# A GRU, convolution and mixture-of-experts kernel: the convolution in 16 pieces with four buffers, and the experts' down products next to the following pair's gate and up products

## The chip, the core and the metric

The kernel runs on one core of a Trainium2 chip. The metric is the device time of one execution in microseconds (us); three runs of the kernel before took 2714.86 to 2716.25 us, with a median of 2714.9 us.

## What is computed

The input x is 128 sequences (b) of 64 steps (t) of 512 features, and cond is 128 rows of 512. Two residual layers follow one another:

```python
# layer 0: a GRU over t that starts from cond, then a linear layer with
# weights rounded to -1, 0, 1 times one scale
x = x + ffn0(gru(cond, x))
# layer 1: a depthwise causal convolution of x along t whose taps are the
# 128 rows of cond, then a mixture of experts with a shared expert
h = conv(x, cond[:, None, :]) + bias
scores = softmax(h @ gate_w.T)              # 64 experts, the best 6 of each row
y = sum over chosen experts of score * ((silu(h @ w_gate[e]) * (h @ w_up[e])) @ w_down[e])
x = x + y + (silu(h @ sw_gate) * (h @ sw_up)) @ sw_down
```

Each expert keeps only the first 64 of the 8192 rows that chose it (CAP); an expert's inner width is 352, the shared expert's is 704. All data are float32.

## The kernel before

TensorE (PE) runs through five stages one after the other.

**The recurrence** (the loop over t at L444). In each step PE multiplies the state by the recurrent weights (L457), adds the input gates of later steps from a stream of products that needs the input weights wih and the bias bi (L311, Strassen-like products for two steps at a time), and applies the rounded linear layer to the state of the step before (ffn, L383). ffn adds the result to x (L398), and SyncE (SP) stores this x1 twice: into out (L408) and into x1c (L400), a scratch array in DRAM ordered as [slice of features][time, reversed][b][features of the slice]. DS is the number of features in one half of a slice, and a row of x1 goes to x1c in runs of DS numbers. In the steps from 2 on, toeplitz (L127) lays out the taps of one half slice in a second scratch array, tzd. The input weights, bi and the other weights are in one pool of on-chip memory, w0, which lives until the loop's end.

**The convolution** (L538 to L574). It is a product of x1c with a Toeplitz matrix of the taps, slice by slice: 8 slices (NSL) of 2 x 32 features. A slice needs two tiles: xc, 2 MB of x1c, and tz, 1 MB of tzd, the two halves of whose partitions are loaded by two DMAs (load_toeplitz, L139, one on SP's queue and, except for slice 1, one on ScalarE's (ACT's)); the rest of tz is cleared once by GpSimd (POOL) (clear, L118). There are two pairs of such tiles, used in turn. The first is made at the start; its first slice is loaded within the recurrence, late rows at step 61 (L406 and L410). The second pair is made after the recurrence, in memory that the recurrence's pools have given up (L535). A slice has 8 groups of 8 matmuls with 64 columns of stationary data each (conv_group, L155); VectorE (DVE) evicts a group with two additions of the bias into hid (L554). Four groups of slice 0 are computed before the last steps of the recurrence are through (L489 to L497). The last two time steps enter by another way: tail_products (L528) and an addition per slice on DVE (L566), from tiles xl and tap that POOL loads. After slice 6, and after slice 7, SP stores the first four steps of hid to the table tab (L573).

**Routing and the shared expert's first half** (L917 to L1024), then **slot counting** (L1098), then **the routed experts together with the shared expert's second half** (L1303 to L1322). In this last stage the shared expert's work comes as a stream of small pieces, and after each of them as many pieces of the routed experts follow as a counter makes due (L1317). Experts are taken in 32 pairs; expert_pair (L1227) has four pieces a pair:

- inputs: the pair's gathered rows are transposed on PE (L1241) and copied by DVE to xeT;
- gate and up: 8 matmuls each into pg and pu (L1253), 64 columns of stationary data for one expert, 64 for the other; ACT's silu and DVE's products make a (L1262); POOL issues the gather of the pair after next (L1216);
- turn: a is transposed on PE (L1267) and copied to aeT;
- down: 6 matmuls into py (L1277), again in halves of 64 columns; ACT copies py to ys (L1285, two buffers), and POOL adds ys to out by two scatters (L1287), the second of which waits until the first has landed.

load_expert (L1065) loads wg, wu and wd of the following pair on SP's queue, which is in order; four experts have buffers. SP also loads xr, the shared expert's rows, after POOL's additions to out (L914) have let its buffer go (L1042).

What a queue does first is set by a scheduler that follows program order and the waits of each tile, and that can move an instruction past others; the order that it made is read from the built program.

Of the kernel before, what the change touches and what calls it, by code (L numbers as in the profile page):

```python
# [8 lines left out]
F32 = mybir.dt.float32  # L9
# [10 lines left out]
P = 128  # L20
B = 128
# [11 lines left out]
DS = 32  # L33
# [9 lines left out]
def adaln_ffn_kernel(  # L43
# [78 lines left out]
    conv_buffers(0)  # L122
# [4 lines left out]
    def toeplitz(q):  # L127

        i = nc.sync.dma_start(
            out=tzd[q],  # L130
            in_=bass.AP(taps.tensor, taps.offset + q * DS * 2 * T, [[1, T], [2 * T, DS], [1, T]]),
        )
        tc.keep_in_program_order(i)

        nc.sync.dma_start(
            out=x1c[q, :TAIL].rearrange("s (r b) e -> (s r) (b e)", r=8), in_=zrow[: 8 * TAIL, :D]
        )

    def load_toeplitz(sl):  # L139

        for hf, queue in enumerate((nc.sync, nc.sync if sl == 1 else nc.scalar)):
            queue.dma_start(out=tzs[sl % 2][hf * T : (hf + 1) * T, hf], in_=tzd[2 * sl + hf])

    TAIL = 2
    LAST = 16

    def load_early(sl):
        for hf in range(2):
            nc.sync.dma_start(
                out=xcs[sl % 2][hf * T + LAST : (hf + 1) * T], in_=x1c[2 * sl + hf, LAST:]  # L150
            )
# [3 lines left out]
    def conv_group(sl, g, ps, parts=2):  # L155
# [3 lines left out]
        for j in range(4):  # L159
            for r in range(parts):  # L160
# [3 lines left out]
                    xcs[sl % 2][:, rows, g * 4 + j],  # L164
                    tzs[sl % 2][:, :, g * 4 + j, :],
# [14 lines left out]
    with (  # L180
# [29 lines left out]
        scale = w0.tile([P, 1], F32, name="scale")  # L210

        bi = w0.tile([P, 3 * D], F32, name="bi")
        wih = [w0.tile([P, KD, D], F32, name=f"wih{c}") for c in range(3)]
# [28 lines left out]
        zrow = w0.tile([NPAD, TW], F32, name="zrow")  # L242
# [4 lines left out]
        ones = w0.tile([P, P], F32, name="ones")  # L247
# [6 lines left out]
        def prepare(c):  # L254
# [4 lines left out]
            t1 = w0.tile([P, HK, HD], F32, name=f"t1{c}")  # L259
            nc.vector.tensor_sub(t1, w12, w11)  # L260
            t2 = w0.tile([P, HK, HD], F32, name=f"t2{c}")
            nc.vector.tensor_sub(t2, w22, t1)
            nc.vector.tensor_sub(w12, w22, w12)
            t4 = w0.tile([P, HK, HD], F32, name=f"t4{c}")
# [118 lines left out]
        def ffn(t, pieces):  # L383
# [20 lines left out]
            if t == T - 1 - TAIL:  # L404
                for hf in range(2):
                    nc.sync.dma_start(out=xcs[0][hf * T : hf * T + LAST], in_=x1c[hf, :LAST])  # L406

            (nc.gpsimd if t >= T - TAIL else nc.sync).dma_start(out=out_t[t], in_=x1)  # L408
            if t == T - 1 - LAST:
                load_toeplitz(0)  # L410
                load_early(0)
# [12 lines left out]
        part = w0.tile([P, T], F32, name="part")  # L424
# [3 lines left out]
        total = w0.tile([P, 1], F32, name="total")  # L428
# [4 lines left out]
        half = w0.tile([P, 1], F32, name="half")  # L433
        nc.vector.tensor_scalar(half, scale, EPS, 0.5, ALU.add, ALU.mult)
        nhalf = w0.tile([P, 1], F32, name="nhalf")
# [8 lines left out]
        for t in range(T):  # L444
# [4 lines left out]
            if t == 1:  # L449
                clear(0)  # L450
            if 2 <= t < 2 * NSL + 2:
                toeplitz(t - 2)
            ps_g = []
# [81 lines left out]
    conv_buffers(1)  # L535
    clear(1)
    cb_h = cb.rearrange("p (q h d) -> p q h d", h=2, d=DS)
    with tc.tile_pool(name="ps_c", bufs=4, space=PSUM) as ps_c:  # L538
        for sl in range(NSL):

            if sl >= 1:
                load_toeplitz(sl)
            if sl >= 1:
                nc.sync.dma_start(
                    out=xcs[sl % 2], in_=x1c[2 * sl : 2 * sl + 2].rearrange("h s b e -> (h s) b e")
                )
# [15 lines left out]
            if sl >= 1:  # L562
                if sl == 1:
                    tail_products()
                d = slice(0 if sl == 1 else 2 * DS * sl, 2 * DS * (sl + 1))
# [4 lines left out]
            if sl >= NSL - 2:  # L570
                d = slice(0, 2 * DS * (NSL - 1)) if sl == NSL - 2 else slice(2 * DS * (NSL - 1), D)
# [493 lines left out]
    def load_expert(e):  # L1065
        wex = wexs[e % 4]
        wg = wex.tile([P, KD, EI], F32, name="wg")
        load_rows(wg, w_gate[e])
        wu = wex.tile([P, KD, EI], F32, name="wu")
        load_rows(wu, w_up[e])  # L1070
        wd = wex.tile([P, len(ech), D], F32, name="wd")
        load_rows(wd[:, :efull, :], w_down[e, : efull * P, :])
        nc.sync.dma_start(out=wd[:n_last, efull, :], in_=w_down[e, efull * P :, :])
        return wg, wu, wd

    weights = {e: load_expert(e) for e in range(4)}
# [150 lines left out]
    def expert_pair(q):  # L1227

        for e in (2 * q + 2, 2 * q + 3):
            if 4 <= e < NE:  # L1230
                weights[e] = load_expert(e)
        rows = gathered.pop(q)
        ws = [weights.pop(2 * q + j) for j in range(2)]


        rw = ex.tile([P, 1], F32, name="rw")
        for j in range(2):
            nc.vector.tensor_copy(rw[halves[j]], rows[halves[j], D + 2 * q + j : D + 2 * q + j + 1])
        ps = ps_e.tile([P, D], F32, name="py").rearrange("p (k b) -> p k b", k=KD)
        for k in range(KD):  # L1240
            nc.tensor.transpose(ps[:, k, :], rows[:, k * P : (k + 1) * P], ident)  # L1241
        xeT = ex.tile([P, KD, P], F32, name="xeT")
        nc.vector.tensor_copy(xeT, ps)
        yield

        if q + 2 < NPAIR:
            gathered[q + 2] = gather(q + 2)
        pg = ps_e.tile([P, EI], F32, name="pg")
        pu = ps_e.tile([P, EI], F32, name="pu")
        for which, acc in ((0, pg), (1, pu)):  # L1250
            for k in range(KD):
                for j in range(2):
                    nc.tensor.matmul(  # L1253
                        acc[halves[j]],
                        xeT[:, k, halves[j]],
                        ws[j][which][:, k, :],
                        start=(k == 0),
                        stop=(k == KD - 1),
                    )
        a = ex.tile([P, EI], F32, name="a")  # L1260
        nc.scalar.activation(a, pg, AF.Silu)
        nc.vector.scalar_tensor_tensor(a, a, rw, pu, ALU.mult, ALU.mult)  # L1262
        yield

        ps = ps_e.tile([P, D], F32, name="py").rearrange("p (k b) -> p k b", k=KD)
        for c, (i0, n) in enumerate(ech):
            nc.tensor.transpose(ps[:n, c, :], a[:, i0 : i0 + n], ident)  # L1267
        aeT = ex.tile([P, len(ech), P], F32, name="aeT")
        nc.vector.tensor_copy(aeT[:, :efull, :], ps[:, :efull, :])
        nc.vector.tensor_copy(aeT[:n_last, efull, :], ps[:n_last, efull, :])  # L1270
        yield


        py = ps_e.tile([P, D], F32, name="py")
        for c, (i0, n) in enumerate(ech):
            for j in range(2):
                nc.tensor.matmul(  # L1277
                    py[halves[j]],
                    aeT[:n, c, halves[j]],
                    ws[j][2][:n, c, :],  # L1280
                    start=(c == 0),
                    stop=(c == len(ech) - 1),
                )
        ys = ex.tile([P, D], F32, name="ys")
        nc.scalar.copy(ys, py)  # L1285
        for j in range(2):
            nc.gpsimd.indirect_dma_start(  # L1287
                out=out,
                out_offset=bass.IndirectOffsetOnAxis(
# [82 lines left out]
```

## Time and profile before

| | |
|---|---|
| median of 3 runs | 2714.9 us |
| the profiled execution's own time | 2715.43 us |
| its span | 2713.7 us |
| recurrence, up to PE's last product of ffn | 0 to 1413.5 us |
| convolution, up to PE's last psc | to 1503.4 us |
| routing, shared expert's first half, slot counting | to the first pair's pg at 2071.4 us |
| routed experts with the shared expert's second half | to 2636 us |
| rest of the shared expert | to the end |
| mean granted clock of PE | 0.994 |

The span runs from the first to the last instruction of the profiled execution. In a row of the timeline stand the start, the time from the first start to the last end, engine, line, operation, what is written and what is read, the form and the count; in brackets is the idle time of the engine before it and what ended it. A float32 matmul gives two records, so x64 is 32 matmuls. In a row of the windows there follow on the stretch and its length the busy time (and count) of PE, PEld (weight loads of PE), DVE, ACT and POOL, then PE's granted clock as a share of full speed, the mean busy share of the 16 DMA engines, and the GB/s that they moved.

### The profile page before, as it was taken

Reading aid. Unit: us, or ns where it says so; the run is one execution under the profiler, and the core shown is the slowest. Engines: PE = TensorE matmul, PEld = TensorE weight load, DVE = VectorE, ACT = ScalarE, POOL = GpSimd, SP = SyncE. Lnnn points to the kernel's source line nnn. Section 1 sums busy time; section 2 is a strip of 40 time slices with the busy share of each in tenths; the row PEclk is TensorE's granted clock in tenths of the full one; section 3 lists DMA queues with packets and bytes.
Section 4 is the critical chain, followed back from the end, with each engine's and each line's share of the span. In section 5 each row is a group of like instructions: output and inputs, shape, how many; then the busy total and the mean of one; then the engine's idle time right before and its main releaser. Section 6 shows DMA issues by size and latency. Waiting matters only on the chain. (4 is left out here: it accounts for less than half of the span.)

```text
span 2713.7 us, 31088 instructions
## 1 busy us (share of the span) xinstructions
PE 2664.6 (98%) x11935; PEld 1827.5 (67%) x11935; DVE 1416.9 (52%) x3143; ACT 426.3 (16%) x794; POOL 425.1 (16%) x471
## 2 busy tenths in 40 slices
PE   8999999999999999999997999999999999999999
PEld 5666666666666666666667767777876666666667
DVE  6555555555555555555555755556564333433334
ACT  1111111111111111111110222222221111111111
POOL 2111111111211111111110000000002222222120
PEclk9999999999999999999998999999999999999999
DMA  5323221111211111311148631222256898998962
GB/s 190 89 71 87 75 66 51 43 51 43 57 53 47 51 43 51 66 51 46 52 112 265 248 94 22 41 58 59 61 174 178 274 321 236 316 322 259 284 181 47
DMA packets 329363, 328.02 MB, mean 121 GB/s; under 512 B 184384, under 2 KB 250432, under 8 KB 327040
## 3 DMA queue, kind: packets, MB, share of 16 engines
q1 hardware_dynamic: 302672, 255.52, 30.9%
q0 software_dynamic: 25984, 66.86, 10.5%
q10 hardware_dynamic: 560, 3.67, 0.6%
q8 instruction: 94, 1.54, 0.2%
q14 instruction: 53, 0.43, 0.1%
HBM read 239.73 MB, written 94.65 MB: 123 GB/s over the span
## 5 line engine op out<-in xcount | busy, mean ns | idle before, releaser
L457 PE MATMUL psgh<-whh,hT 128*128 128x512 f32 x1536 | 674.6, 595 | 0.7 <-ACT hT L372 0.7
L457 PEld LDWEIGHTS psgh<-whh,hT 128*128 128x128 f32 x1536 | 286.6, 190 | 350.2 <-issue 336.3
L311 PE MATMUL psx<-wih,xp 128*128 128x256 f32 x768 | 198.5, 381 | 6.8 <-DMA wih<-in_w_ih_dram 6.6
L200 POOL DMA_DIRECT2D xn<-in_x_dram x61 | 34.0, 558 | 853.4 <-DVE x L398 841.8
L311 PEld LDWEIGHTS psx<-wih,xp 128*128 128x128 f32 x768 | 143.7, 191 | 26.5 <-issue 6.6
L467 DVE TENSOR_TENSOR n<-psgh,bhn 128x512 f32<-128x512 f32 x64 | 44.3, 692 | 175.5 <-PE psgh L457 175.5
L372 ACT COPY hT<-psf 128x512 f32<-128x512 f32 x64 | 37.5, 586 | 584.8 <-PE psf L366 584.8
L464 DVE TENSOR_TENSOR r<-psgh,gi 128x512 f32<-128x512 f32 x64 | 44.3, 692 | 139.2 <-PE psgh L457 139.2
L386 POOL TENSOR_TENSOR xn<-xn,fb 128x512 f32<-128x512 f32 x64 | 80.8, 1264 | 143.9 <-DMA xn<-in_x_dram 143.9
L311 PE MATMUL psz<-wih,xs 128*128 128x256 f32 x384 | 98.7, 379 | 1.8 <-DVE gi L334 1.8
L311 PE MATMUL psy<-t,xs 128*128 128x256 f32 x384 | 99.9, 383 | 0.1
L311 PE MATMUL psw<-wih,xp 128*128 128x256 f32 x384 | 99.4, 381 | 0.0
L311 PE MATMUL psw<-t,xp 128*128 128x256 f32 x384 | 98.8, 380 | 0.4 <-DVE u L332 0.4
L311 PE MATMUL psz<-t,xs 128*128 128x256 f32 x384 | 98.7, 379 | 0.0
L390 PE MATMUL psf<-sgn,hhi 128*128 128x512 f32 x256 | 95.2, 493 | 0.0
L1277 PE MATMUL py<-wd,aeT 128*64 128x512 f32 (+1 forms) x384 | 90.6, 601 | 0.0
L1262 DVE SCALAR_TENSOR_TENSOR a<-a,rw,pu 128x352 f32<-128x352 f32 x32 | 18.6, 581 | 136.8 <-PE pu L1253 136.8
L162 PE MATMUL psc<-tz,xc 128*64 128x128 f32 x960 | 68.2, 310 | 20.6 <-DMA xc<-x1c 17.8
L326 DVE TENSOR_TENSOR p<-psx,bi 128x512 f32<-128x512 f32 x96 | 66.4, 692 | 37.3 <-PE psx L311 37.0
L1287 POOL DMA_INDIRECT out_dram<-ys,idxp x32 | 45.5, 1421 | 250.4 <-ACT ys L1285 202.7
L647 PE MATMUL psx<-xr,swg 128*128 128x256 f32 x320 | 84.3, 385 | 0.0
L647 PE MATMUL psx<-hid,swg 128*128 128x256 f32 x320 | 84.1, 386 | 0.1
(298 smaller groups left out, 4672.5 us busy)
## 6 DMA issues: line engine op xcount, KB each, us to landing
wg<-in_w_gate_dram SPq DMA_DIRECT2D x64, 704.0 KB, 8.0
wu<-in_w_up_dram SPq DMA_DIRECT2D x64, 704.0 KB, 10.5
wd<-in_w_down_dram SPq DMA_DIRECT2D x64, 512.0 KB, 8.9
x1c<-x SPq DMA_DIRECT2D x62, 256.0 KB, 4.2
out_dram<-x SPq DMA_DIRECT2D x62, 256.0 KB, 4.5
xn<-in_x_dram POOLq DMA_DIRECT2D x61, 256.0 KB, 4.0
xp<-in_xT_dram POOLq DMA_DIRECT2D x30, 512.0 KB, 4.4
tab<-hid SPq DMA_DIRECT2D x60, 256.0 KB, 3.7
```

The lines of the kernel that those rows point to most:

```text
L162: i = nc.tensor.matmul(ps[rows, j], xcs[sl % 2][:, rows, g * 4 + j], tzs[sl % 2][:, :, g * 4 + j, :], start=True, stop=True,)
L311: i = nc.tensor.matmul(ps, self.ops[n][:, k, :], self.ws[n][:, k, :], start=(first and k == 0), stop=(k == HK - 1), skip_group_check=not f ...
L326: add(self.p1, both, b)
L372: nc.scalar.copy(hT, ps)
L386: nc.gpsimd.tensor_add(xn, xn, fb)
L390: nc.tensor.matmul(ps, piece[:, k, :], sgn[:, k, :], start=(i == 0 and k == 0), stop=(i == 1 and k == KD - 1),)
L457: nc.tensor.matmul(ps, hT[:, k, :], whh[c][:, k, :], start=(k == 0), stop=(k == KD - 1))
L464: nc.vector.tensor_add(r, ps_r, gis.pop((t, 0)))
L467: nc.vector.tensor_add(n, ps_n, bhn)
L647: nc.tensor.matmul(ps.rearrange("p (j b) -> p j b", b=P) if len(r.shape) == 3 else ps, lhs(k), r, start=(first and k == 0), stop=(k == HK ...
L1277: nc.tensor.matmul(py[halves[j]], aeT[:n, c, halves[j]], ws[j][2][:n, c, :], start=(c == 0), stop=(c == len(ech) - 1),)
L1287: nc.gpsimd.indirect_dma_start(out=out, out_offset=bass.IndirectOffsetOnAxis(ap=(idxp[:CAP] if j == 0 else idxo)[:, q : q + 1], axis=0), i ...
```

## The change

The change has two parts that do not touch each other's stages.

First, DS goes from 32 to 16, so there are 16 slices (here "pieces") of half the size, and there are four pairs of tiles (NCB) instead of two, each of half the size. Two pairs are made at the start. The other two are made in step 62 (t == T - TAIL), after a new pool, wi, has been closed that holds bi, the input weights and their sums; other small tiles move ahead of it into w0. Pieces 0 and 1 are loaded as slice 0 was; pieces 2 and 3 are loaded whole at the place where slice 0's late rows are loaded. From piece 4 on load_piece(sl) stands at the start of loop iteration sl, and its tiles are those of piece sl - 4. Stores to x1c have runs of 16 numbers, toeplitz runs in 32 steps instead of 16, the tail's products come with piece 4, and the stores of hid to tab come after pieces 13 and 15.

Second, the pieces of a pair of experts become methods, and experts() orders them anew: turn(q), then inputs(q + 1), then down(q) and gate_up(q + 1) as one piece. Weights of pair q + 2 are loaded in two calls, gate and up in turn(q), down in down(q). The counter spreads 97 pieces over the same stretch of the shared expert as 128 before.

The core of the diff:

```diff
-DS = 32
+DS = 16
...
-    conv_buffers(0)
+    NCB = 4
+    for i in range(2):
+        conv_buffers(i)
...
     def load_toeplitz(sl):
 
-        for hf, queue in enumerate((nc.sync, nc.sync if sl == 1 else nc.scalar)):
-            queue.dma_start(out=tzs[sl % 2][hf * T : (hf + 1) * T, hf], in_=tzd[2 * sl + hf])
+        for hf, queue in enumerate((nc.sync, nc.sync if 2 <= sl < NCB else nc.scalar)):
+            queue.dma_start(out=tzs[sl % NCB][hf * T : (hf + 1) * T, hf], in_=tzd[2 * sl + hf])
...
+    def load_piece(sl):
+        load_toeplitz(sl)
+        nc.sync.dma_start(
+            out=xcs[sl % NCB], in_=x1c[2 * sl : 2 * sl + 2].rearrange("h s b e -> (h s) b e")
+        )
...
+        wi_ = ExitStack()
+        wi = wi_.enter_context(tc.tile_pool(name="wi", bufs=1))
+
+        bi = wi.tile([P, 3 * D], F32, name="bi")
+        wih = [wi.tile([P, KD, D], F32, name=f"wih{c}") for c in range(3)]
...
             if t == T - 1 - TAIL:
-                for hf in range(2):
-                    nc.sync.dma_start(out=xcs[0][hf * T : hf * T + LAST], in_=x1c[hf, :LAST])
+                for sl in range(2):
+                    for hf in range(2):
+                        nc.sync.dma_start(
+                            out=xcs[sl][hf * T : hf * T + LAST], in_=x1c[2 * sl + hf, :LAST]
+                        )
+                for sl in range(2, NCB):
+                    load_piece(sl)
...
             if t == T - 1 - LAST:
-                load_toeplitz(0)
-                load_early(0)
+                for sl in range(2):
+                    load_toeplitz(sl)
+                    load_early(sl)
...
             if t == 1:
                 clear(0)
+                clear(1)
             if 2 <= t < 2 * NSL + 2:
                 toeplitz(t - 2)
+            if t == T - TAIL:
+                wi_.close()
+                for i in range(2, NCB):
+                    conv_buffers(i)
+                    clear(i)
...
-    conv_buffers(1)
-    clear(1)
...
-            if sl >= 1:
-                load_toeplitz(sl)
-            if sl >= 1:
-                nc.sync.dma_start(
-                    out=xcs[sl % 2], in_=x1c[2 * sl : 2 * sl + 2].rearrange("h s b e -> (h s) b e")
-                )
+            if sl >= NCB:
+                load_piece(sl)
...
-            if sl >= 1:
-                if sl == 1:
+            if sl >= NCB:
+                if sl == NCB:
                     tail_products()
...
-            if sl >= NSL - 2:
-                d = slice(0, 2 * DS * (NSL - 1)) if sl == NSL - 2 else slice(2 * DS * (NSL - 1), D)
+            if sl in (NSL - 3, NSL - 1):
+                d = slice(0, 2 * DS * (NSL - 2)) if sl == NSL - 3 else slice(2 * DS * (NSL - 2), D)
...
+    def load_gate_up(q):
+
+        if q < NE // 2:
+            for e in (2 * q, 2 * q + 1):
+                wg = wexs[e % 4].tile([P, KD, EI], F32, name="wg")
+                load_rows(wg, w_gate[e])
+                wu = wexs[e % 4].tile([P, KD, EI], F32, name="wu")
+                load_rows(wu, w_up[e])
+                weights[e] = [wg, wu]
+
+    def load_down(q):
+        if q < NE // 2:
+            for e in (2 * q, 2 * q + 1):
+                wd = wexs[e % 4].tile([P, len(ech), D], F32, name="wd")
+                load_rows(wd[:, :efull, :], w_down[e, : efull * P, :])
+                nc.sync.dma_start(out=wd[:n_last, efull, :], in_=w_down[e, efull * P :, :])
+                weights[e].append(wd)
...
+        pairs = [Pair(q) for q in range(NPAIR)]
+        pairs[0].inputs()
         yield
+        pairs[0].gate_up()
         yield
+        for q, pair in enumerate(pairs):
+            pair.turn()
+            yield
+            if q + 1 < NPAIR:
+                pairs[q + 1].inputs()
+                yield
+            pair.down()
+            if q + 1 < NPAIR:
+                pairs[q + 1].gate_up()
+            yield
...
-            while due < 4 * NPAIR and due * PIECES * SPREAD < slot * 16 * NPAIR:
+            while due < EPIECES and due * PIECES * SPREAD < slot * 4 * EPIECES:
                 next(routed)
                 due += 1
```

The methods of Pair hold the same instructions as the pieces of expert_pair; turn() also calls load_gate_up(q + 2), and down() calls load_down(q + 2) between its products and the copy to ys. EPIECES is 3 * NPAIR + 1.

## The prediction, made before the change was timed

> **What bounds the kernel now.** I read the page's first two parts, then TensorE's (PE's) timeline where its row of tenths dips, then a table of windows over the same stretch.
>
> ```profile
> PE 2664.6 (98%) x11935; PEld 1827.5 (67%) x11935; DVE 1416.9 (52%) x3143; ACT 426.3 (16%) x794; POOL 425.1 (16%) x471
> ...
> PEclk9999999999999999999998999999999999999999
> ```
>
> PE is busy for 98%, so time falls only where PE idles (49 us in all), runs at a lower granted clock, or is busy with less than it could do. The convolution has the first two:
>
> ```profile
> 1419.76 4.19 PE L162 MATMUL psc<-tz,xc 128*64 128x128 f32 x64 [1.02 <-POOL tz L120]
> 1425.72 4.35 PE L162 MATMUL psc<-tz,xc 128*64 128x128 f32 x64 [1.77 <-DVE hid L554]
> 1433.28 18.69 PE L162 MATMUL psc<-tz,xc 128*64 128x128 f32 x256 [3.21 <-DMA xc<-x1c]
> 1458.31 18.22 PE L162 MATMUL psc<-tz,xc 128*64 128x128 f32 x256 [6.34 <-DMA xc<-x1c]
> 1484.75 18.68 PE L162 MATMUL psc<-tz,xc 128*64 128x128 f32 x256 [8.22 <-DMA xc<-x1c]
> ```
>
> A slice is 128 records (64 matmuls of two), so the last three rows are two slices each. PE ends at 1503.43; before them stand 20.6 us of idleness, 17.8 of it for a load of xc. The windows show why:
>
> ```profile
> 1445.20:1466.90 21.70, 15.36 (x215) 15.20 (x214) 10.27 (x29) 0.00 (x0) 0.00 (x0) 0.84 0.93 291
> 1466.90:1469.80 2.90, 2.90 (x51) 2.90 (x50) 2.36 (x8) 0.00 (x0) 0.00 (x0) 1.00 0.02 6
> 1469.80:1492.60 22.80, 14.58 (x198) 14.41 (x197) 9.46 (x26) 0.00 (x0) 0.00 (x0) 0.78 0.91 277
> 1492.60:1503.50 10.90, 10.83 (x171) 10.64 (x168) 8.25 (x24) 0.00 (x0) 0.00 (x0) 1.00 0.24 87
> ```
>
> The last three columns are clock, DMA share and GB/s. Two slices' loads (6.29 MB) take some 22 us at 277 to 291 GB/s, and then the DMA engines stand still until PE frees a buffer. PE and DMA take turns, and after each wait PE runs at half clock (the trace has it for 6.8, 6.8 and 10.2 us).
>
> The experts are different: PE never idles, but pays on changing between the full array and two halves of 64 columns.
>
> ```profile
> 2094.78 0.81 PE L647 MATMUL psz<-es,st 128*128 128x256 f32 x3
> 2095.52 2.80 PE L1277 MATMUL py<-wd,aeT 128*64 128x512 f32 x12
> 2098.24 1.13 PE L647 MATMUL psx<-xr,swg 128*128 128x256 f32 x4
> 2099.21 1.03 PE L647 MATMUL y<-es,st 128*128 128x256 f32 x4
> 2100.07 0.60 PE L1241 MATMUL py<-ident,rows 128*128 128x128 f32 x4
> ```
>
> A full-array block of four records normally takes 0.86 us from its start to the next one's (y: 2099.21 to 2100.07); the block psx after the halves takes 0.97.
>
> **Convolution: 16 pieces, four buffers.** Matmuls, evictions and bytes stay the same; a piece is 64 records, 1.57 MB and four groups.
>
> *Before the stage.* x1 is stored to x1c in runs of 64 B, not 128, so 4096 packets a step instead of 2048. This store of step 61 gates the first loads. In the trace it is issued at 1391.63 and has landed by 1394.97, of which packets take 2.0 us (13 to 16 ns each). At the same price per packet it takes 2 us more. The Trainium skill (DMA: Bandwidth & Descriptors, Specifications) speaks against the change: under 512 B an engine does a read-modify-write and loses line rate. The old 128 B packets are under that already, so the row should contain it; if each shorter packet cost twice as much, the store would be late by 6 us. PE first needs this data at 1405.85, and the tail loads (issued 1394.97) landed in 5.0 us, at 1400: slack 5.8 us. So I take zero; the bound is from zero to 1 us. The other 61 stores have no reader near and lie under a PE that is full.
>
> toeplitz runs 32 times at half size on SP, during recurrence steps in which SP mostly waits for x. The four memsets of buffers 2 and 3 now stand on POOL in step 62, after the last xn addition and ahead of the tap loads and the last stores of x. They wait for PE's last use of the input weights (1378.3) and take 4 x 0.9 = 3.6 us: done by 1383, while those stores wait until 1407. Zero, and the 1.02 us wait for POOL is gone. On SP four loads of tz wait for the same PE point, ahead of the step-61 store (1391.6): zero. tail_products moves to piece 4, where DVE's wait for xl (landed by 1422.2) is covered by pieces 2 and 3 in hand; the 1.77 us goes too.
>
> *The stage.* Pieces 0 to 3 are loaded or loading at the start, as slices 0 and 1 were: those 3.1 MB landed at 1411.7 before, 1413 now. PE ends the early groups, which are exactly piece 0, at 1414.6, so piece 4 can be issued then instead of at 1418.77. First packets come 1.8 us after the issue, 1416.4 (1418.77 to 1420.57 in the trace). From there loads follow each other without a stop, since with four buffers three are always queued. Price: 22.4, 21.7 and 22.8 us per four pieces, each including a start; I take 5.4 us a piece (bounds 4.6, at 340 GB/s, and 5.8). Tap, xl and x traffic of 0.8 MB adds 2.6. So piece s lands at 1419 + 5.4 x (s - 3), piece 13 at 1473, 14 at 1478.4. PE takes 4.0 to 4.2 us a piece at full clock: it waits from about piece 7 on, some 1.3 us each time.
>
> The clock: the Trainium skill (TensorE: Matmul & The Clock Gate, Part 1) says it halves after an idle window of about 3.4 us. The rows: full clock after waits of 1.02 and 1.77 us, half after 3.21, 6.34 and 8.22. Waits of 1.3 us are nearest the first two: full clock. By a harsher reading [...] pieces would take up to 8 us; PE would then be full and the clock return, so at most about 4 us.
>
> *A wait that the change adds.* In the built order SP issues the last tz load, then four stores tab<-hid (448 columns), then xc of piece 15. The stores wait for the evictions of piece 13; before, they stood behind all loads. Piece 13 ends on PE at 1477.5, on DVE at 1478.5; four stores take 1.8 us of SP (1495.85 to 1497.64 in the trace); xc follows at 1480.9, starts at 1482.7 and, behind 0.9 MB of stores and with 1 MB of its own, lands near 1486. PE ends piece 14 at 1482.9, waits 3 us, and ends piece 15 at 1490.3 (up to 1.7 later if the clock falls). Without those stores it would be 1488. What follows (stores, weight loads, the first transposes) keeps its distance from this end. Gain: 1503.4 - 1490.8 = **12.6 us**, bounds 6 and 19.
>
> **Experts: down of q next to gate and up of q+1.** From single records' starts in the trace: in a run of full-array records each starts 216 ns after the last; into halves it is 309 (93 more); the first pair of halves takes 50 more than the steady 430 or 296; out of halves 97 to 100 more; the second full record 320 (104 more). Together 345 ns a stretch, and py shows the same as pg with pu. Before there are 65 such stretches (32 gate-up, 31 down and one split in two), in the built order after there are 33: "py6 pg8 pu8" 31 times without anything between. 32 x 345 ns = **11.0 us**. All of it is on PE, which is full there.
>
> Cover: two or three shared products still stand between turn, inputs and down, as two do now with no wait in the rows, so copies of aeT, xeT and ys stay hidden. Weight loads keep their order in effect: SP already issues wg and wu after the pair's pu and wd after its down. DMA share is 0.92 to 0.94 there and rises 2%. On POOL a gather now stands behind both scatters of a pair, so 7 us later; its rows are needed more than a pair (15.3 us) on. Bound for the whole part: 7 to 11.5; I take 10.5.
>
> **Sum.** 12.6 + 10.5 = 23 off the span of 2713.7: 2690.7. The profiled execution took 2715.43; the median, 2714.9, is 1.2 above the span. So 2692.
>
> **Rivals.**
> - *PE-bound convolution* (7 in 100): the queues overlap tz and xc so that data keeps pace (windows of 350 to 390 GB/s occur). PE then ends near 1482; with experts -32: 2683. Against: no whole reload ran above 291.
> - *The loads stay the limit* (17 in 100): half-size rows (8 and 4 KB) or the late xc cost as much as the removed pauses (2.9 us each) gave. Convolution gains 3 to 6, total -15: 2700.
> - *The switch isn't saved* (10 in 100): halves with other row counts or a stall on weights cost what was won. Total -12: 2703. Against: inside py the step from 128 to 96 rows costs nothing.
> - *Slower: POOL's scatter chain* (5 in 100). Each scatter waits for the one before to land:
>
> ```profile
> 2184.93 1.44 POOL L1287 DMA_INDIRECT out_dram<-ys,idxo  x1 [4.08 <-DMA out_dram<-ys,idxp]
> 2192.19 1.45 POOL L1287 DMA_INDIRECT out_dram<-ys,idxp  x1 [5.83 <-DMA out_dram<-ys,idxo]
> 2193.94 1.01 POOL L1216 DMA_INDIRECT rows<-tab,idxp  x1 [0.30 <-PE psw L647]
> 2199.77 1.42 POOL L1287 DMA_INDIRECT out_dram<-ys,idxo  x1 [4.82 <-DMA out_dram<-ys,idxp]
> ```
>
> A pair needs 14.8 us (2184.93 to 2199.77) of PE's 15.7, soon 15.3. If denser loads and the gather push it past 15.3, two ys buffers fill and ACT, then PE, wait. It cancels the gain at 16.0 (32 x 0.72 = 23 us); at 16.3, landing times 10% longer than now, the kernel is 32 us behind the forecast: 2724.
>
> The likeliest case has 58 in 100, no effect 3. Its own range is 2685 to 2698; over the rivals 2683 to 2704. A measurement tells 0.2% (5.4 us) from nothing: faster 0.90, within 0.05, slower 0.05.
>
> **What will show it.** Right: PE's waits for xc of 1 to 2 us from piece 7 on, one near 3 before the last; DMA share above 0.9 from 1417 to 1480 without a pause; PE's last psc near 1490; py-pg-pu runs without 128*128 rows between, pair period 15.3. Wrong: a first psx later than 1406, half clock during the pieces, PE idle for wg or wd, ys waiting for a scatter.

## The result, and the profile after

| | before | after |
|---|---|---|
| median | 2715.6 us (4 runs) | 2699.0 us (4 runs, 2698.3 to 2701.3) |
| ratio after to before, 95% interval | | 0.9940 (0.9923 to 0.9958) |
| profiled execution: its time, its span | 2715.4, 2713.7 us | 2699.1, 2697.0 us |
| convolution: first psx to PE's last psc | 97.3 us | 93.4 us |
| first pst to the first pg | 567.0 us | 566.1 us |
| first pg to the last py of the experts | 564.0 us | 551.5 us |
| from there to PE's last record | 73.6 us | 74.5 us |

The kernel is faster by 16.6 us, 0.6%. The forecast was 2692 with a range of 2683 to 2704. The four stretches in the table (starts of PE's records in the two traces) say where the difference lies: 3.9 us in the convolution, 0.9 behind it, 12.5 in the experts, of which 0.9 comes back at the end; the convolution also starts 0.5 us earlier. The limits of the last three shift a little with the order: in the kernel after, two shared full-array records (0.43 us) more stand ahead of the first pg, and four (0.86 us) more behind the last py. At equal work the stretch behind the convolution is 1.3 us shorter and that of the experts 11.2 us. The convolution was to give 12.6.

The first two parts of the page after. PE is busy for the same 98%, and the tenth of the granted clock that fell short before is gone:

```profile
PE 2647.6 (98%) x11935; PEld 1825.2 (68%) x11935; DVE 1414.2 (52%) x3148; ACT 426.1 (16%) x794; POOL 425.2 (16%) x475
...
PEclk9999999999999999999999999999999999999999
```

PE's timeline through the convolution of the kernel after:

```profile
1414.94 3.91 PE L170 MATMUL psc<-tz,xc 128*64 128x128 f32 x64 [0.23 <-DVE x L413]
1423.43 25.49 PE L170 MATMUL psc<-tz,xc 128*64 128x128 f32 x384 [4.57 <-DVE hid L571]
1451.06 3.96 PE L170 MATMUL psc<-tz,xc 128*64 128x128 f32 x64 [2.13 <-DMA xc<-x1c]
1458.37 4.06 PE L170 MATMUL psc<-tz,xc 128*64 128x128 f32 x64 [3.35 <-issue]
1465.14 3.99 PE L170 MATMUL psc<-tz,xc 128*64 128x128 f32 x64 [2.72 <-DMA xc<-x1c]
...
1481.80 4.03 PE L170 MATMUL psc<-tz,xc 128*64 128x128 f32 x64 [1.77 <-DMA xc<-x1c]
1486.05 4.00 PE L170 MATMUL psc<-tz,xc 128*64 128x128 f32 x64 [0.23 <-DMA xc<-x1c]
1493.53 5.54 PE L170 MATMUL psc<-tz,xc 128*64 128x128 f32 x64 [3.48 <-DMA xc<-x1c]
```

Three things are to be seen. The waits are short and come one a piece, as forecast, but from piece 8 to piece 13 (the rows from 1451.06 to 1481.80) they are 1.5 to 3.4 us instead of 1.3; piece 14 waits for 0.2. The last wait is there (3.5 us, forecast 3). And a wait of 4.57 us stands at the start that no step of the prediction has: PE waits for DVE. DVE's own timeline and POOL's say for what:

```profile
1417.09 0.42 DVE L571 TENSOR_TENSOR hid<-psc,cb 128x256 f32<-128x256 f32 x1 [0.41 <-PE psc L170]
1421.43 0.42 DVE L571 TENSOR_TENSOR hid<-psx,cb 128x256 f32<-128x256 f32 x1 [3.92 <-DMA out_dram<-x]
```

```profile
1415.18 0.55 POOL L428 DMA_DIRECT2D out_dram<-x  x1 [7.78 <-DVE x L413]
1421.57 0.54 POOL L546 DMA_DIRECT2D xl<-out_dram  x1 [5.84 <-DMA out_dram<-x]
```

The tile hid1 (the later half of the time steps) lies in memory that io0 gave up, and the x1 of steps 62 and 63 are in io0. So DVE's first write into hid1 waits until the store of the last x1 has landed. In the kernel before, that store was issued at 1413.97, and by 1417.32, 3.35 us later, POOL could issue the load that needs it:

```profile
1413.97 0.55 POOL L408 DMA_DIRECT2D out_dram<-x  x1 [6.08 <-DVE x L398]
1417.32 0.55 POOL L523 DMA_DIRECT2D xl<-out_dram  x1
```

Now it is issued at 1415.18, 0.4 us after the loads of pieces 4 and 5 have begun to be issued, and lands at 1421.4, 6.2 us later. PE fills its four psc buffers and stops.

The windows of after show the other half of the story:

```profile
1445.00:1460.00 15.00, 9.52 (x156) 9.20 (x157) 7.85 (x23) 0.00 (x0) 0.00 (x0) 1.00 1.03 281
1460.00:1475.00 15.00, 10.38 (x170) 9.87 (x166) 8.73 (x26) 0.00 (x0) 0.00 (x0) 1.00 1.02 267
```

The DMA engines are busy without a pause (share 1.02 to 1.03) at full clock, as forecast, and yet move only 267 to 281 GB/s, less than the reloads of before that had pauses in them (277 to 291).

The experts look as forecast. PE's timeline of one pair after, where down, gate and up follow one another and a full-array block starts 2.47 us after pu, with no record between:

```profile
2229.85 2.80 PE L1311 MATMUL py<-wd,aeT 128*64 128x512 f32 x12
2232.48 2.54 PE L1285 MATMUL pg<-wg,xeT 128*64 128x352 f32 x16
2234.85 2.54 PE L1285 MATMUL pu<-wu,xeT 128*64 128x352 f32 x16
2237.32 1.13 PE L664 MATMUL psw<-swd,aT 128*128 128x256 f32 x4
```

All 31 such stretches take 7.46 us from the first py to the next full-array record; apart, they took 2.73 and 4.88. That is 0.15 us a stretch; the rest of the forecast's 0.345, 93 ns on the way in and 104 in the second full record behind it, lies outside these times. PE is busy for 250.00 of 250 us from 2250 to 2500. POOL's scatters (its waits, in us in total, times, longest) waited mainly for ys before, and now wait for each other; first the line of before, then three of after:

```profile
POOL out_dram L1287 <- ACT ys L1285: 202.7, 25, 16.0
```

```profile
POOL out_dram L1322 <- DMA out_dram<-ys,idxp: 128.3, 22, 7.4
POOL out_dram L1322 <- DMA out_dram<-ys,idxo: 66.3, 13, 7.0
POOL out_dram L1322 <- ACT ys L1320: 56.3, 10, 7.8
```

### The profile page after: what moved, and what is told of

It reads as the page before. It is cut to its first block, busy times and chain, and to the rows that moved or that the text cites. A ratio compares the mean times of both kernels' runs of the same rounds, so it can differ in the third digit from the quotient of the medians.

```text
span 2697.0 us, 31139 instructions
## 1 busy us (share of the span) xinstructions
PE 2647.6 (98%) x11935; PEld 1825.2 (68%) x11935; DVE 1414.2 (52%) x3148; ACT 426.1 (16%) x794; POOL 425.2 (16%) x475
## 3 DMA queue, kind: packets, MB, share of 16 engines
q0 software_dynamic: 25984, 66.86, 10.5%
## 5 line engine op out<-in xcount | busy, mean ns | idle before, releaser
L493 ACT ACTIVATE n<-n 128x512 f32<-128x512 f32 x64 | 40.3, 629 | 274.0 <-DVE n L492 274.0
```

The costliest lines, as they stand in the source:

```text
L493: nc.scalar.activation(n, n, AF.Tanh)
```

## The experiments

Theories at the start. A: the experts gave what they should, and the convolution lost its gain to the store's late landing and to loads at 6.1 us a piece. The rival for each part is told with the run. A ratio to the kernel before stands with its 95% interval where a kernel was run four times or more; a time without one, in section 5, is a single run with a profile.

**1. The two parts alone.** The first kernel is before with the new experts() alone, the second is after with expert_pair of before.

> The kernel before with the new order of the experts alone. My theory, read from the two traces (experts give 11 to 11.7 us, the convolution 4.4, the smaller clock loss after it about 1): 11 us below before, 2704; 31 stretches py-pg-pu of some 7.46 us from py's start to pu's end in place of two stretches; convolution as before, PE's last psc near 1503. Rival (the experts' part gains only because the loads of the convolution change or because the schedule shifts as a whole, and the parts do not add up): under 7 us or over 14.

> The kernel after with the old order of the experts: 16 pieces and four buffers alone. My theory: PE's last psc near 1499 (4.4 us earlier than before), another 1 us from a shorter half-clock stretch behind it, total 5 to 6 us below before, 2710. Rival (the forecast's size, 12.6 us from the convolution, and the experts gave less than they seem): 2703.

Measured: experts alone 0.9961 (0.9948 to 0.9975), 10.6 us; convolution alone 0.9981 (0.9975 to 0.9988), 5.2 us. Together 15.8 of the 16.3 that the ratio of after gives: the parts add up within their intervals. In the traces the stretch from the first pg to the last py is 564.0 us in every kernel with the old order of the experts and 551.5 or 551.6 in every one with the new, whatever the convolution does. The rivals (the forecast's 12.6 for the convolution; parts that do not add up) fall. One thing came out against my numbers: the kernel with the convolution alone took 96.2 us from the first psx to the last psc, with the same code for it that took 93.4 in after. In this profile only 1.1 us of the gain stand there, and 4.3 stand behind it (first pst to first pg 562.7 us, 567.0 before). The clock moves time between the two: half clock held for 20.5 us of this convolution and for 10.2 of after's, and behind it for nothing here, for 3.4 us in after and for 6.8 before. So what the convolution's part gives is read from both stretches together, 5.4 us in this profile; the last section tells where the half clock comes from.

**2. The store of step 63 ahead of the loads.**

```diff
-            (nc.gpsimd if t >= T - TAIL else nc.sync).dma_start(out=out_t[t], in_=x1)
+            (nc.gpsimd if t == T - TAIL else nc.sync).dma_start(out=out_t[t], in_=x1)
```

> The kernel after, with the last store of x1 (step 63) to out put on SP's queue ahead of piece 4's loads instead of on POOL's behind them. Theory A (the 4.57 us that PE waits for DVE in the convolution come from this store's late landing: hid of step 1 uses its memory again, and the store shares the DMA engines with the loads of pieces 4 and 5): the store lands 2 to 3 us earlier, DVE's first addition into hid is on time, PE's wait falls to under 2 us, the clock stays full at 1423 to 1429, piece 6 is issued up to 7 us earlier and the last psc comes 3 to 6 us earlier; total 2693 to 2696. Theory B (the DMA stream alone sets the end, and a gap at 1427 to 1431 only moves the waits): total within 1.5 us of after, with the later waits for xc longer by as much.

Measured: 0.9965 (0.9952 to 0.9979), so no faster than after (0.9940, 0.9923 to 0.9958), and by the medians 4.8 us slower. The store landed 4.6 us after its issue instead of 6.2, and the first wait fell; but PE and DVE show a new one:

```profile
1423.36 6.47 PE L170 MATMUL psc<-tz,xc 128*64 128x128 f32 x80 [2.52 <-DVE hid L571]
1435.80 24.16 PE L170 MATMUL psc<-tz,xc 128*64 128x128 f32 x368 [5.96 <-DVE hid L571]
```

```profile
1434.29 0.69 DVE L552 TENSOR_TENSOR tap<-tap,xl 128x512 f32<-128x512 f32 x1 [8.55 <-DMA xl<-out_dram]
```

POOL's load of xl can only start when the store has landed, and took 12.5 us against the loads of pieces 4 and 5 (8.3 in after). DVE comes to the tail's product earlier than in after, waits 8.55 us for xl, and the evictions of piece 2 from its second group on are queued behind it. The order that DVE was given has changed too: the product stands three groups earlier in it than in after. So the cover of tail_products that the prediction named was itself made by the first wait. Neither theory had this; the chain is store, load of xl, product, evictions.

**3. No store and no load in the chain.** The x1 of steps 62 and 63 are written straight into xl, so that hid1 waits for neither store and POOL loads no xl.

```diff
-            x1 = io0.tile([P, D], F32, name="x1")
+            x1 = xls[0][:, t - (T - TAIL)] if t >= T - TAIL else io0.tile([P, D], F32, name="x1")
...
+                xls.append(
+                    conv.enter_context(
+                        tc.tile_pool(name="xlp", bufs=1, side="right", reuse_waits="tile")
+                    ).tile([P, TAIL, D], F32, name="xl")
+                )
...
-    xl = tail.tile([P, TAIL, D], F32, name="xl")
-    nc.gpsimd.dma_start(out=xl, in_=out_t[T - TAIL :].rearrange("t b d -> b t d"))
+    xl = xls[0]
```

> The kernel after, with x1 of the last two steps (62 and 63) written straight into xl, a tile that is made in step 62 next to buffers 2 and 3. So hid's first write into the old io0 memory waits for no store of these steps, and POOL's load of xl is gone, with the wait that took the place of the first one when the store was only put earlier. Theory A (the DVE wait of 4.57 us comes from the stores of steps 62 and 63): no DVE wait above 1 us in the convolution, full clock from 1414 to at least 1445, piece 6 issued by 1424 instead of 1430, DMA share above 0.8 all through 1417 to 1485, last psc 2 to 6 us earlier than after; total 2693 to 2697. It is no more than that since 11 pieces at 6.1 us each from 1416.4 end at 1483.5, against some 1485.5 in after. Theory B (the DVE wait only took the place of a wait for loads, and costs nothing by itself): total within 1.5 us of after.

Measured: 0.9939 (0.9925 to 0.9952), median 2697.6. PE's timeline has the wait gone:

```profile
1414.93 19.18 PE L170 MATMUL psc<-tz,xc 128*64 128x128 f32 x320 [0.27 <-DVE xl L413]
1435.33 4.00 PE L170 MATMUL psc<-tz,xc 128*64 128x128 f32 x64 [1.22 <-DMA xc<-x1c]
1442.12 5.49 PE L170 MATMUL psc<-tz,xc 128*64 128x128 f32 x64 [2.79 <-DMA xc<-x1c]
```

Five pieces run without a break, and piece 14 starts at 1482.15 instead of 1486.05. So the cause of the 4.57 us is shown, and in this profile the wait cost 3.9 us of the convolution. The times show less: the span is 2.9 us shorter in the profile, the medians differ by 1.4, and the two ratios are the same within their intervals. Theory A holds for the cause. The total lies just above A's range and within B's 1.5 us of after, so how much of the 3.9 us the kernel keeps is not shown.

**4. The stores of hid to tab after the last piece.**

```diff
-            if sl in (NSL - 3, NSL - 1):
-                d = slice(0, 2 * DS * (NSL - 2)) if sl == NSL - 3 else slice(2 * DS * (NSL - 2), D)
+            if sl == NSL - 1:
                 for t in range(4):
-                    nc.sync.dma_start(out=tab_t[t, :, d], in_=hid(t)[:, d])
+                    nc.sync.dma_start(out=tab_t[t, :, :D], in_=hid(t))
```

> The kernel after, with all four stores of hid to tab in one go after the last piece, so that none stands ahead of piece 15's xc on SP. Theory A (the stores delay xc of piece 15 and cost 3.5 us of waiting and 1.5 us of half clock): PE waits under 0.5 us before its last 64 records, which take 4.0 us instead of 5.54; the last psc 3 to 5 us earlier; but tab's stores are then four of 512 columns after the end, up to 1.5 us later for whoever reads tab; the first gather is hundreds of us on, so nothing comes back: total 2694 to 2696. Theory B (piece 15's xc would not land earlier since the DMA engines are full with piece 14 and 15's tz until then): last psc at most 1 us earlier, total 2698 to 2699.

Measured: 0.9934 (0.9920 to 0.9948), median 2694.7, 4.3 us under after. The last piece:

```profile
1490.82 4.04 PE L170 MATMUL psc<-tz,xc 128*64 128x128 f32 x64 [0.20 <-PE psc L170]
```

A wait of 0.2 us and full clock, against 3.48 us and half clock in after; PE's last psc starts 4.2 us earlier. Theory A stands by the profile and the median; the intervals of the two ratios overlap. With both repairs, of sections 3 and 4:

> The kernel after with both repairs that helped alone in their profiles: x1 of steps 62 and 63 written straight into xl, and the four stores of hid to tab in one go after the last piece. If the two waits are separate losses (my theory): no DVE wait above 1 us at the start, the last wait for xc under 1.5 us, last psc 4.2 and 4.2 us earlier than after added up, near 1490.5, total 2689 to 2693. If both draw on the same slack of the loads: last psc near 1494, total 2694 to 2696.

Measured: 0.9921 (0.9907 to 0.9934), median 2693.2; the convolution takes 87.7 us from the first psx to the last psc, 5.7 less than in after. It lies between the two cases: the two waits share part of their cost, since the loads behind them stay the limit.

**5. What makes a piece cost 6.1 us.** Three kernels, each run once, and then a pair. First the size of rows: before, with each load split in two so that rows are as long as in after.

> The kernel before (two buffers, 8 slices) with each tz and each xc load split in two DMAs, so that rows are 4 KB and 8 KB as in after. It changes the size of rows alone. Theory A (the halved rows cost the DMA rate, as the rival with the loads as limit said): a reload of two slices takes 24 to 25 us instead of 22, each of the three waits for xc is 2 us longer, total 2720 to 2724. Theory B (the size does not matter at 4 and 8 KB): reloads within 0.7 us of before, total within 3 us of before.

Measured: 2712.1 us, convolution 95.3 us against 97.3 in before. Halved rows cost nothing, so that half of the rival forecast ("half-size rows cost as much as the removed pauses") falls. In three windows of this kernel loads of xc, then of tz, then of xc make up most of the packets:

```profile
1460.00:1465.00 5.00, 5.00 (x83) 4.97 (x81) 3.89 (x11) 0.00 (x0) 0.00 (x0) 1.00 1.03 342
1465.00:1470.00 5.00, 2.90 (x35) 2.55 (x36) 1.69 (x5) 0.00 (x0) 0.00 (x0) 1.00 1.01 223
1470.00:1475.00 5.00, 5.00 (x86) 5.00 (x85) 3.87 (x11) 0.00 (x0) 0.00 (x0) 1.00 1.00 341
```

The same share of DMA moves 342 or 223 GB/s, by what is loaded. Next, without tz loads, and with all of tz on SP's queue:

> The kernel after without the tz loads of pieces 4 to 15; those pieces are computed with the taps of pieces 0 to 3, so part of the result is left out. It measures what one xc load costs when no tz load is mixed in. Theory A (mixing tz, of 64 partitions and 4 KB rows, with xc slows both: 495 ns for an 8 KB packet against some 310 alone): 8 KB packets at 310 to 330 ns, a piece's 1.05 MB in 2.5 to 2.7 us, PE never waits for xc after piece 5, last psc near 1483. Theory B (8 KB rows of xc are slow by themselves, or slow beside a busy PE): packets stay at 450 to 500 ns, and 1.05 MB take 3.9 us; PE is then about even with the loads.

> The kernel after with both halves of tz loaded from SP's queue instead of one half from ACT's. Theory A (two queues whose packets interleave on the DMA engines slow each other): packets of 8 KB fall from 495 to under 400 ns, GB/s from 261-283 to over 310, PE's waits for xc fall under 1 us each, last psc 4 or more us earlier. Theory B (the mix of kinds or the rows' sizes set the rate, not the number of queues): the same GB/s within 5 percent; the last psc up to 2 us later, since SP's order holds one more DMA.

Without tz (pieces from 4 on use old taps, so the kernel leaves their own out): 2679.1 us, and PE's 896 records from 1422.53 on have no wait among them:

```profile
1422.53 54.27 PE L171 MATMUL psc<-tz,xc 128*64 128x128 f32 x896 [4.09 <-DVE hid L572]
```

The median 8 KB packet from 1432 to 1482 takes 309 ns, where it took 461 in after. With one queue: 2707.3 us, 235 to 244 GB/s in the windows from 1445 to 1475, and a last wait of 7.34 us, which is slower than either theory had it. So it is tz beside xc, and not that there are two queues. What distinguishes tz? Each of its loads writes 64 neighbouring partitions, 0 to 63 or 64 to 127; an xc load writes 128. Two kernels test that. In the first, xc is also split in two loads of 64 neighbouring partitions. In the second, both tz and xc are split in two loads of every second partition (which partition holds which row changes, in both alike; the early loads go the same way, and tz is cleared as one block):

```diff
-            queue.dma_start(out=tzs[sl % NCB][hf * T : (hf + 1) * T, hf], in_=tzd[2 * sl + hf])
+            queue.dma_start(out=tzs[sl % NCB][hf : 2 * T : 2, hf], in_=tzd[2 * sl + hf])
...
-        nc.sync.dma_start(
-            out=xcs[sl % NCB], in_=x1c[2 * sl : 2 * sl + 2].rearrange("h s b e -> (h s) b e")
-        )
+        for hf in range(2):
+            nc.sync.dma_start(out=xcs[sl % NCB][hf : 2 * T : 2], in_=x1c[2 * sl + hf])
```

> The kernel after with each xc load split in two DMAs, of partitions 0-63 and 64-127, and nothing else: the same number of DMAs as the interleaved kernel, without the interleaving. Theory A (the rate goes with the spread of partitions that one load writes): 8 KB packets of xc rise from 495 to 520 ns or more, GB/s fall under 260, last psc 3 to 12 us later than after. Theory B (the split is free; the mix or tz's source set the rate): the same packets and GB/s within 5 percent.

> The kernel after with the two halves of a piece interleaved over the partitions: half hf of tz and of xc goes to partitions hf, hf+2, and so on up to 126+hf, in one DMA each of 64 rows with a step of two, instead of to partitions 0-63 or 64-127. Bytes and row sizes stay; xc has two DMAs a piece instead of one. Theory A (a load that writes a block of 64 neighbouring partitions moves at about half the rate of one that writes 128: tz rows of 4 KB take 245 to 275 ns, 240 GB/s, and slow the xc packets beside them to 500 ns; xc alone takes 309 ns; the loads of 48 partitions at 1095 us took 690 to 770 ns per 8 KB): tz packets fall to under 200 ns, xc to under 350 ns, a piece to about 4.2 us, PE's waits for xc between pieces vanish, DMA share falls under 0.95, last psc at 1483 to 1488, total 2682 to 2690. Theory B (the slowness comes from the source of tz, from the taps' scratch array, or from two kinds of loads mixed, wherever they go): the same 255 to 285 GB/s as after, packets within 10 percent, last psc within 2 us, total within 3 us of after.

Measured: neighbouring halves 2720.5 us, slower than before (2712.4 to 2718.0 beside it); interleaved 2684.1 us, ratio 0.9885 (0.9870 to 0.9901). The window from 1445 to 1460, first of the halves, then of the interleaved kernel:

```profile
1445.00:1460.00 15.00, 8.80 (x124) 8.66 (x126) 5.18 (x15) 0.00 (x0) 0.00 (x0) 0.89 1.02 213
```

```profile
1445.00:1460.00 15.00, 15.00 (x254) 14.88 (x253) 12.35 (x35) 0.00 (x0) 0.00 (x0) 1.00 1.02 413
```

The same number of DMAs with the same rows and bytes move 213 or 413 GB/s. The times of single packets in the traces, by how many tz packets were in flight meanwhile (at most 20 were; 1432 to 1482 in after, 1416 to 1482 in the two others):

| mean (median) ns of a packet | tz, 4 KB, 13 or more tz in flight | xc, 8 KB, fewer than 1.5 tz | xc, 8 KB, 4 to 7 tz |
|---|---|---|---|
| after | 263 (274) | 391 (342) | 505 (506) |
| halves | 301 (296) | 616 (638) | 622 (640) |
| interleaved | 244 (159) | 342 (309) | 326 (313) |

A load into 64 neighbouring partitions is slow (halves: everything is), and one of all 128 that runs beside it is slowed too (after: 391 to 505). Interleaved, neither happens: of all its tz packets three quarters take 160 ns or less. Theory A of this pair stands. Three of its numbers missed: the DMA share stayed at 1.02 where under 0.95 was expected, piece 14 still waited 3.41 us, and the last psc of the halves came 21.5 us later than in after, not 3 to 12.

The Trainium skill has a reason (SBUF — State Buffer, Door 1: The DMA port swizzle): a transfer's rate goes with how many of 16 ports its partitions reach, and partitions 0 to 63 reach 8 of them, for at most about 218 GB/s. The 213 and 222 GB/s of the halves are close to that. By the same section's mapping every second partition reaches all 16, which fits the 413 GB/s of the interleaved kernel; that the ports are the cause no trace here shows by itself. The section "Can I just issue two DMAs to hit both halves?" of that page says that only one transfer over all 128 partitions reaches all the ports. The 413 GB/s with loads of 64 partitions each differ from that, and the measurement decides.

**6. All three repairs.**

> The kernel after with the three repairs: halves interleaved over the partitions, x1 of steps 62 and 63 written straight into xl, and the stores of hid to tab in one go after the last piece. My theory (packets of 160 and 310 to 330 ns, so that a piece's loads take some 3.9 us against 4.0 to 4.3 us of PE; no DVE wait at the start; no late xc at the end): PE is busy almost without a break from 1415 to the last psc near 1479 to 1481, no wait above 1.5 us, the clock full throughout, 4 us earlier than the interleaved kernel alone; total 2679 to 2682. Rival (with the loads at 410 GB/s the two other waits are covered by buffers in hand, or the loads and DVE's evictions now set the pace): total 2682 to 2686, as the interleaved kernel.

Measured: 2677.0 us (2674.7 to 2679.1), ratio 0.9861 (0.9845 to 0.9878): 22 us under after and 38 under before. PE's timeline of the whole convolution:

```profile
1415.24 19.18 PE L168 MATMUL psc<-tz,xc 128*64 128x128 f32 x320 [0.27 <-DVE xl L411]
1436.17 4.01 PE L168 MATMUL psc<-tz,xc 128*64 128x128 f32 x64 [1.74 <-DMA xc<-x1c]
1440.46 26.49 PE L168 MATMUL psc<-tz,xc 128*64 128x128 f32 x448 [0.29 <-DMA tz<-tzd]
1468.96 7.78 PE L168 MATMUL psc<-tz,xc 128*64 128x128 f32 x128 [2.01 <-DMA xc<-x1c]
```

The convolution takes 70.8 us from the first psx to the last psc (97.3 before), with two waits of 1.7 and 2.0 us, and the clock is full until the last 0.5 us of the span. The two other repairs, which gave 5.7 us in the profile while the loads were the limit, now give 6.6 more than interleaving alone (77.4). My theory stands, though both waits are longer than its 1.5 us and the time is 2 us below its range.

## Why the prediction was right and wrong

**Right.** The sign, and the range, the latter with some luck: 2699.0 lies outside the likeliest case's own 2685 to 2698 and inside the whole range only because that covers the rivals, and 2 us from elsewhere made up for a part of what the convolution lacked, which gave 4.4 us against a lower bound of 6. The experts are right in mechanism and size: 32 stretches less at 345 ns are 11.0 us, of which 10.5 was taken; the stretch from the first pg to the last py is 12.5 us shorter, of which 0.86 us (four shared records that now come behind it) and 0.43 (two that now come ahead of it) are moved work: 11.2. The scatter chain, the rival on the slower side, did not decide: POOL's waits for landings rose and PE did not wait. Before the stage: the tail loads behind the x1c store were issued 0.8 us later (forecast 2, bounds 0 to 6, no effect; a 64 B packet of this store took 9.6 ns in the mean where a 128 B one took 12.6, so none cost twice as much), the memsets took 3.9 us under cover, the 1.02 us for POOL is gone. The clock: waits of up to 3.35 us kept it full. The added wait for piece 15: 3.48 us and a piece of 5.54 us; forecast 3 and up to 1.7 late by the clock. Its price by itself was forecast as 2.3 us (1490.3 against 1488) and is 4.2.

**Wrong: the 12.6 us of the convolution.** PE's last psc ended at 1499.1, not 1490.3 (the sum takes 1490.8, half a microsecond more than its own text). The last piece's xc stands behind the stores to tab, and these behind piece 13; it was issued at 1488.3, not at 1480.9, because the stream of loads was late. Counted at piece 14, which was to land at 1478.4 and came at 1485.9, it was 7.5 us late; the clock in the last piece added the 1.5. Two steps failed.

- "I take 5.4 us a piece": from 1431 to 1486 nine pieces took 54.7 us, 6.07 each: 6.0 us. The step took the rate from reloads in which tz and xc came mostly one behind the other (in before 216 GB/s from 1445 to 1450, where 124 of 148 packets are tz's, and 360 from 1450 to 1455, where 108 of 124 are xc's). With four buffers a load of tz is mostly beside one of xc and slows it (section 5). It also took the shortest of its three reloads: 22.4, 21.7 and 22.8 us are 5.6 a piece in the mean, which would have left 4.4 of the 6.0 us. The upper bound of 5.8 was too low by the same error. The rival "the loads stay the limit" named the right outcome (2700) with a reason that is right in part: the halved rows cost nothing, and the late xc cost 4.2 us.
- "The 1.77 us goes too", with pieces 2 and 3 as cover: it went, and 4.57 us of another wait came. The step named the work that hides DVE's wait for xl, and not what else DVE's first evictions wait for. The store of step 63 is not touched by the change; what was not seen is that piece 4's loads, issued earlier, take the DMA engines from it (it landed after 6.2 us behind them, and after 4.6 ahead of them in section 2). So piece 6's buffer came free late, and between the last packet of piece 5 at 1427.4 and the first of piece 6 at 1431.3 no load of a piece was under way: 3.9 us of the stream (DMA share 0.61 from 1425 to 1430). Against these two stands 2.4 us: pieces 4 and 5 landed at 1427.4, not at 1429.8.

6.0 + 3.9 - 2.4 = 7.5 us. The end of the convolution came 4.4 us earlier than before (0.5 of it from ahead of the stage) instead of 12.6. Those are 8.2 us too few. Less the experts' 0.7 above the forecast and the 1.3 behind the convolution that the sum did not have, that is 6.2 of the 6.3 us by which the span, 2697.0, lies above the forecast 2690.7.

## What to carry to other kernels

When a prefetch is put earlier, list every other transfer that is in flight at that moment, stores too, and ask who waits for its landing; a tile that takes over old memory waits for the last store out of it. Price a stream of mixed loads from rows in which they are mixed, and not from rows in which they take turns. And look at which partitions a load writes: two loads that each write every second partition moved 413 GB/s here, where two that each write one half moved 213.

## What was not expected of the hardware

The half-clock stretches of a run all begin on one grid of 3.41 us (in before 1432.3, 1456.2, 1480.1 and 1517.6, apart by 7, 7 and 11 such steps). In the traces of all fourteen kernels, from 1340 us to the last psc, every step at full clock in which PE was busy for 0.41 of the time or less was followed by one at half clock, and none with 0.45 or more was; between these both occur (0.42 and 0.44 once each before half clock, 0.42 to 0.44 four times before full). Behind the convolution there was one exception, 0.54 and then half clock. So the same wait costs nothing or half a step's work, by where it falls: the wait of 3.35 us in after, split over two steps, kept the clock. The recurrence, the same code in all, shows it best. A wait of 1.7 us and one of 0.7 us at 1390 left the clock full in after, and half in the kernel with the earlier store; the line that follows in each:

```profile
1393.14 10.57 PE L480 MATMUL psgh<-whh,hT 128*128 128x512 f32 x24 [0.68 <-ACT hT L387]
```

```profile
1393.30 12.21 PE L480 MATMUL psgh<-whh,hT 128*128 128x512 f32 x24 [0.67 <-ACT hT L387]
```

That is 1.6 us for the same code. Such steps are also why the convolution took 93.4 us in one profile and 96.2 in another with the same code, and why differences of 2 to 3 us between single profiles are read here only beside the waits that explain them. The Trainium skill (TensorE: Matmul & The Clock Gate, Part 1) has the window of 3413 ns and that it runs freely; the share at which it decides is from these traces.
